# Softmax sums and degrees from a feature set to one, rows turned ahead of their products, and the second expert bias moved into the slots

## The chip, the cores and the metric

The kernel runs on one core of one Trainium2 chip. The metric is the device time of one execution in microseconds (us), the median of several runs. The engines of a core work side by side, each through its own list of instructions: TensorE (PE in the profile, its weight loads PEld), VectorE (DVE), ScalarE (ACT), GpSimd (POOL) and the DMA queues, which are fed from SyncE (SP), ACT and POOL. SBUF is the memory on the core, PSUM the banks into which TensorE writes, DRAM the memory outside.

## What is computed

Four layers with residual sums on 3125 nodes of 256 features and 100,000 edges that are sorted by target node, in float32. The rows are padded to 25 blocks of 128 (3200).

```python
x = x + gnn0(layernorm(x))     # two graph attention layers, 4 heads and 1 head
x = x + ffn0(layernorm(x))     # mixture of 8 experts, 2 chosen for all rows
x = x + gnn1(layernorm(x))     # linear, then two graph convolutions
x = x + ffn1(layernorm(x))     # mixture of 8 experts, 2 chosen for each row

# first attention layer, per head k
h  = x @ W1                                     # 256 -> 4 * 256
e  = leaky_relu((h . a_src)[src] + (h . a_dst)[dst])
w  = exp(e - max of e over the edges into dst)  # a self loop for each node too
out[dst] = sum(w * h[src]) / sum(w)

# graph convolution
deg[dst] = number of edges into dst, plus 1
x  = relu(sum(x[src] @ W / sqrt(deg[src] * deg[dst])) + b)

# last layer, for row n and its two experts e with shares s
y[n] = sum over e of s[n, e] * (gelu(ln_e(x[n]) @ W1[e] + b1[e]) @ W2[e] + b2[e])
```

## The kernel before, in words

`FirstLayer` computes the first attention layer on raw normalised features: the weighted sums of x are made first, and multiplied by W1 afterwards. Its `run` (L2093) begins with a head: it loads all rows, normalises them in groups of five blocks (`norm_rows`, L1541), writes them to a DRAM `table`, multiplies W1 with the attention vectors (`attention_vectors`, L1561), turns every block with PE (L2140), and multiplies each turned block by those vectors (L2148). The scores go to DRAM (`table`, `terms`, `loops`).

Then one loop (L2185) drives three jobs side by side, so many steps of each per turn of the loop. PE, DVE and ACT keep the written order (`in_order`); SP and POOL are ordered by the compiler's scheduler from the dependences.

- Counting (`count_step`): for each of 391 chunks of 256 edges, one-hot tiles are made (L1669 to L1678), multiplied on PE (L1686), and added to a piece of the matrix of edge counts (L1703, L1708). The piece changes nine times (L1659).
- Edges (`edge_step`): for the 283 chunks whose targets lie above node 256. POOL gathers the source rows (L1797, twelve chunks ahead); four chunks are a batch. Per batch, DVE makes the one-hot of target places (`edge_hot`, L1820), the weights `edge_p` (L1840 to L1844), and their product `edge_moves` (L1849), which holds for each row 4 heads x w places, w being 14 or 20. Per chunk, PE multiplies the gathered rows by `edge_moves` for two halves of the features (L1863), and then multiplies `edge_p`, with a fifth column of ones, by `edge_hot` (L1869): that gives the four softmax sums and the degree in five rows. DVE adds the ninefold result to `agg` (L1880): 8 sets of feature sums, and a ninth that is used in its first five rows.
- Dense heads (`dense_step`): targets below 256 are done from the counts, 25 steps a head; `rows` has a 257th column of ones, which gives the sum (L2045).

`agg` covers 384 target nodes at a time, in eight pieces. Work on a finished piece is put in a queue of tasks, and each turn of the loop does one. `new_sums` (L1905) clears a piece and sets the self loops (L1933, and a transpose L1938 and copy L1939 for the ninth set). `through_w1` (L1956) takes the reciprocal of the four sums on four partitions (L1967, L1968), sends it through DRAM so that every partition has it (`by_node`, L1970 and L1975), scales the eight sets (L1982), and multiplies by W1 (L1989). After the last chunk, the last piece's steps up to scaling are put in front of the queue (L2198).

The last layer (`Router`) sends rows to slots. `tasks` (L2311) chooses the experts of each block during the second convolution; its `begin` (L2415) multiplies a block's shares by the experts' second bias (transpose L2419, copy L2421, product L2423, DVE add L2424) and writes the block to the output. The slots (`load`, `front`, `slot`, L2556 to L2638) then each load the weights of one expert, do 256 rows, multiply by the share (L2630), and add the rows to the output by an indirect DMA (L2631). Weights are loaded two slots ahead. Five of the 25 `begin`s run within the first slots.

Of the kernel before, what the change touches and what calls it, by code (L numbers as in the profile page):

```python
# [36 lines left out]
CH = [(c, min(c + 512, NP)) for c in range(0, NP, 512)]  # L37
GB = 5
# [50 lines left out]
class Kernel:  # L89
    def __init__(self, ctx, tc):  # L90
# [10 lines left out]
        self.rows = const.tile([P, NB, D + 1], F32, name="x_rows")  # L101
        self.x = self.rows[:, :, :D]
# [1291 lines left out]
class FirstLayer:  # L1394
# [10 lines left out]
    def __init__(self, k, I):  # L1405
# [8 lines left out]
        self.inverse = k.dram.tile([AS, 4, GA], F32, name="inverse")  # L1414
# [126 lines left out]
    def norm_rows(self, x, to, pool):  # L1541
# [3 lines left out]
        for b in range(GB):  # L1545
            st = pool.tile([P, 6], F32, name="ln0_st", bufs=3)
            nc.vector.bn_stats(st, x[:, b, :])
            nc.vector.bn_aggr(mv[:, b, :], st)
        yield
# [5 lines left out]
        for b in range(GB):  # L1555
            nc.scalar.activation(x[:, b, :], x[:, b, :], AF.Identity, bias=rstd[:, 1, b:b + 1],
                                 scale=rstd[:, 0, b:b + 1])
# [19 lines left out]
    def first_terms(self, sd, pool):  # L1577
# [32 lines left out]
        self.own = pool.tile([P, NB - DB, n + 1], F32, name="own_w")  # L1610
        own = self.own[:, :, :n]
# [4 lines left out]
        nc.vector.memset(self.own[:, :, n:], 1.0)  # L1616
# [136 lines left out]
    def open_sums(self, ctx, w1, stats):  # L1753
# [3 lines left out]
        self.ps_out = ctx.enter_context(tc.tile_pool(name="ps_po1", bufs=DB, space=PSUM, reuse_waits="tile"))  # L1757
# [8 lines left out]
        self.probs = [work.tile([P, BT, 5], F32, name=f"edge_p{i}") for i in range(2)]  # L1766
        for p in self.probs:
            nc.vector.memset(p[:, :, 4:], 1.0)
        self.spread = [work.tile([P, BT * 4 * CW + EW], F32, name=f"edge_moves{i}")
                       for i in range(2)]  # L1770
# [18 lines left out]
        self.hot_e, self.agg = {}, {}  # L1789
        self.ready, self.later = 0, []  # L1790
# [21 lines left out]
    def place_edges(self, m):  # L1812

        nc, work = self.nc, self.work
        n, w = self.size[m], width(C0 + m * BC)
        h = self.hot_e[m] = work.tile([P, BT * CW], F32, name="edge_hot", bufs=3)[
            :, :n * CT * w].rearrange("p (t w) -> p t w", w=w)
# [5 lines left out]
        nc.vector.tensor_scalar(t[:k, :], t[:k, :], self.part[:k, :], None, op0=ALU.is_equal)  # L1823

# [10 lines left out]
    def weigh_edges(self, m):  # L1835
        nc, n = self.nc, self.size[m] * CT
        p = self.probs[m % 2][:, :n, :4]
# [8 lines left out]
    def spread_edges(self, m):  # L1846
        n, w = self.size[m] * CT, width(C0 + m * BC)
        shape = [P, n, 4, w]
        self.nc.vector.tensor_tensor(  # L1849
            self.spread[m % 2][:, :n * 4 * w].rearrange("p (t k w) -> p t k w", k=4, w=w), self.hot_e[m][:, :, None, :].to_broadcast(shape),  # L1850
            self.probs[m % 2][:, :n, :4, None].to_broadcast(shape), ALU.mult)

    def multiply_edges(self, c):
# [6 lines left out]
        for f in range(2):  # L1860
            for u in range(CT):
# [3 lines left out]
                                 rhs=self.spread[m % 2][:, e * 4 * w:e * 4 * w + EW],  # L1865
                                 start=(u == 0), stop=(u == CT - 1))
        for u in range(CT):
            e = q * CT + u
            nc.tensor.matmul(ps[:5, 8 * w:9 * w], lhsT=self.probs[m % 2][:, e, :],  # L1869
                             rhs=self.hot_e[m][:, e, :], start=(u == 0), stop=(u == CT - 1))  # L1870
# [34 lines left out]
    def new_sums(self, q):  # L1905
# [4 lines left out]
        def clear():  # L1910
            a = self.agg[q] = self.work.tile([P, 9, GA + EXT], F32, name="agg1", bufs=2)
            self.nc.vector.memset(a[:, :, n:], 0.0)
            self.nc.vector.memset(a[:, 8, :n], 0.0)
            load(0)
# [12 lines left out]
        def loops(i):  # L1927
            nc, a, k = self.nc, self.agg[q], self.k
# [8 lines left out]
            pt = self.aux.tile([P, 512], F32, name="aux")  # L1937
            nc.tensor.transpose(pt[:5, :P], self.own[:, blocks[i] - DB, :], k.ident)  # L1938
            nc.scalar.copy(a[:5, 8, ts(i, P)], pt[:5, :P])  # L1939
# [16 lines left out]
    def through_w1(self, q):  # L1956
# [5 lines left out]
        inv = []  # L1962

        def invert():
            nc.sync.dma_start(self.deg_row.rearrange("b p -> (b p)")[None, n0:n0 + n],
                              a[4:5, 8, :n])
            nc.vector.tensor_scalar(a[:4, 8, :n], a[:4, 8, :n], 1e-30, None, op0=ALU.max)  # L1967
            nc.vector.reciprocal(a[:4, 8, :n], a[:4, 8, :n])  # L1968

            nc.sync.dma_start(self.inverse[q, :, :n], a[:4, 8, :n])  # L1970

        def load():
            for i in range(0, n, P):
                w = self.work.tile([P, 4 * P], F32, name="by_node", bufs=3)
                nc.sync.dma_start(w.rearrange("p (k n) -> p k n", k=4),  # L1975
                                  self.inverse[q, :, i:i + P][None].to_broadcast([P, 4, P]))
                inv.append(w)

        def scale(i):
            v = a[:, :8, ts(i, P)].rearrange("p (c k) n -> p c k n", c=2)  # L1980
            w = inv[i].rearrange("p (k n) -> p k n", k=4)
            nc.vector.tensor_tensor(v, v, w[:, None].to_broadcast([P, 2, 4, P]), ALU.mult)  # L1982

# [9 lines left out]
        return ([invert, load, lambda: None] + [lambda i=i: scale(i) for i in range(n // P)]  # L1993
# [13 lines left out]
    def open_dense(self):  # L2007
        self.steps = [(h, j) for h in range(4) for j in range(NB)]
        self.cnts, self.t_rows, self.zs, self.ws, self.pos = {}, {}, {}, {}, {}
# [29 lines left out]
    def multiply_dense(self, s):  # L2039
        h, j = self.steps[s]  # L2040
        w = self.ws.pop(s)
        for i in range(DB):
            if j == 0:
                self.pos[i] = self.ps_out.tile([P, 512], F32, name="po")
            self.nc.tensor.matmul(self.pos[i][:, :D + 1], lhsT=w[:, ts(i, P)],  # L2045
                                  rhs=self.k.rows[:, j, :], start=(j == 0), stop=(j == NB - 1))
        if j == NB - 1:
            turned = self.work.tile([P, 2, DN], F32, name="turned")
            for i in range(DB):
                self.dense_end(i, self.pos[i], turned)  # L2050
# [3 lines left out]
    def dense_end(self, i, po, turned):  # L2054
        nc = self.nc
        inv = self.work.tile([P, 1], F32, name="inv", bufs=4)
        nc.vector.tensor_scalar(inv, po[:, D:D + 1], 1e-30, None, op0=ALU.max)
# [692 lines left out]
```

## Time and profile before

| what | us |
|---|---|
| median of 3 runs | 2605.72 |
| lowest and highest run | 2597.94, 2615.81 |
| the profiled execution | 2613.59 |
| its span in the trace | 2611.8 |
| busy in the span: PE, PEld | 2244.2, 1809.0 |
| busy in the span: DVE, ACT, POOL | 1375.9, 1150.3, 821.3 |

The span runs from the first to the last instruction of the trace; the profiled execution's own time is 1.8 us longer. Busy times are averages over stages that differ; the stages are read from stretches of the trace. The head lies from 0 to about 105 us, the loop of the first layer to 1078, its last products to 1112, the second attention layer to about 1500, the chosen experts of the first mixture to about 1720, the convolutions to about 2180, and the slots to the end. The mean granted TensorE clock is 0.904 of full speed. A row such as `L1869 ... x4` stands for merged records; one float32 product has two records, and the bracket at the end of a row gives the idle time before it and what ended it.

### The profile page before, as it was taken

How to read it: one execution, taken by the hardware profiler on the slowest of the kernel's cores; microseconds unless marked ns; L12 is line 12 of the kernel's file. 1: busy time of each engine (PE TensorE's matmuls, PEld its weight loads, DVE VectorE, ACT ScalarE, POOL GpSimd, SP SyncE). 2: the span in 40 equal slices, each digit the busy share in tenths (PEclk: the TensorE clock that was granted, in tenths of full speed). 3: DMA queues.
4: the chain of work that ended last, by engine and by line, in shares of the span. 5: the costliest groups of instructions: out<-in, count | busy, mean ns of one | idle time of the engine just before them, and what ended most of it. 6: DMA issues, size and time to landing. Idle time of an engine off the chain costs nothing. (4 is left out here: it accounts for less than half of the span.)

```text
span 2611.8 us, 38442 instructions
## 1 busy us (share of the span) xinstructions
PE 2244.2 (86%) x11731; PEld 1809.0 (69%) x11731; DVE 1375.9 (53%) x4343; ACT 1150.3 (44%) x2553; POOL 821.3 (31%) x800
## 2 busy tenths in 40 slices
PE   4377878788878888678999979988999998999996
PEld 4255666666656665467888858876877676788886
DVE  7666556466667676613888844342334666111110
ACT  3267555545555555351444424444433444222221
POOL 1555566566566677020000030000000213222221
PEclk8577889888889889889999979999999889799998
DMA  7633445464556556399422110004324435466663
GB/s 231 116 88 84 126 122 169 109 178 114 164 144 181 158 164 177 125 351 304 145 71 76 51 49 1 1 1 139 113 79 155 131 106 195 134 195 196 200 204 77
DMA packets 240363, 354.30 MB, mean 136 GB/s; under 512 B 44640, under 2 KB 181571, under 8 KB 236434
## 3 DMA queue, kind: packets, MB, share of 16 engines
q1 hardware_dynamic: 197122, 252.44, 30.6%
q0 software_dynamic: 39456, 94.80, 14.2%
q10 hardware_dynamic: 3568, 4.47, 0.7%
q8 instruction: 98, 1.61, 0.2%
q14 instruction: 119, 0.97, 0.1%
HBM read 265.94 MB, written 86.20 MB: 135 GB/s over the span
## 5 line engine op out<-in xcount | busy, mean ns | idle before, releaser
L1797 POOL DMA_INDIRECT edge_rows<-table,pick x566 | 604.6, 1068 | 352.2 <-PE edge_sums L1863 139.5
L1863 PE MATMUL edge_sums<-edge_moves,edge_rows 128*128 128x120 f32 x2264 | 357.7, 309 | 36.2 <-DVE agg L1880 23.5
L1863 PEld LDWEIGHTS edge_sums<-edge_moves,edge_rows 128*128 128x128 f32 x2264 | 334.6, 221 | 73.4 <-DVE agg L1880 34.0
L1092 PE MATMUL po<-parts,cnt_r 128*128 128x512 f32 x1250 | 327.7, 416 | 9.5 <-ACT cnt_r L1086 9.5
L1703 ACT CAST acc<-ps 128x325 f32 (+2 forms) x391 | 178.4, 456 | 269.1 <-DVE acc L1708 89.2
L1092 PEld LDWEIGHTS po<-parts,cnt_r 128*128 128x128 f32 x1250 | 240.2, 197 | 69.0 <-ACT cnt_r L1086 10.3
L1686 PE MATMUL ps<-hot_key,hot_lo 128*128 128x350 f16 (+2 forms) x782 | 209.2, 361 | 87.9 <-ACT hot_lo L1678 35.8
L854 PE MATMUL po<-h,w 128*128 128x257 f32 x1250 | 277.6, 382 | 6.7 <-DVE w L845 4.4
L854 PEld LDWEIGHTS po<-h,w 128*128 128x128 f32 x1250 | 236.6, 191 | 43.1 <-DVE w L845 6.4
L1669 DVE TENSOR_SCALAR hot_key<-iota_key,key 128x350 f16<-128x350 f16 (+2 forms) x782 | 231.6, 323 | 24.1 <-PE edge_sums L1863 8.4
L2619 ACT ACTIVATE hid<-ph,ffn_b 128x256 f32<-128x256 f32 (+1 forms) x232 | 105.8, 456 | 278.9 <-PE ph L2617 275.2
L2617 PE MATMUL ph<-xe,ffn_w 128*128 128x256 f32 (+1 forms) x928 | 199.3, 371 | 2.8 <-DMA ffn_w<-in_L_ffn_W 2.8
L2627 PE MATMUL py<-ffn_w,hid 128*128 128x256 f32 x848 | 189.1, 380 | 0.0
L2631 POOL DMA_INDIRECT out<-y,to x53 | 82.6, 1559 | 326.1 <-DVE y L2630 218.0
L2617 PEld LDWEIGHTS ph<-xe,ffn_w 128*128 128x128 f32 x928 | 165.7, 195 | 27.8 <-DVE free L2601 2.9
L2627 PEld LDWEIGHTS py<-ffn_w,hid 128*128 128x128 f32 x848 | 159.2, 191 | 20.4
L839 ACT ACTIVATE z<-z,att_cols 128x640 f32<-128x640 f32 x125 | 103.1, 828 | 152.9 <-DVE z L837 130.1
L1675 ACT ACTIVATE hot_lo<-iota_key,lo 128x128 f16<-128x128 f16 x494 | 169.0, 391 | 0.0
L1880 DVE TENSOR_TENSOR agg<-agg,edge_sums 128x126 f32 (+1 forms) x283 | 87.2, 308 | 148.5 <-remote 41.0
L1686 PEld LDWEIGHTS <-hot_lo 128*128 128x128 f16 x782 | 62.8, 105 | 142.1 <-ACT hot_lo L1678 48.0
L1086 ACT CAST cnt_r<-cnt_h 128x1920 fp32r<-128x1920 f16 x50 | 89.9, 1799 | 136.2 <-PE po L1092 130.8
L2045 PE MATMUL po<-x_rows,w 128*128 128x257 f32 x400 | 128.6, 449 | 2.0 <-issue 2.0
(420 smaller groups left out, 3365.0 us busy)
## 6 DMA issues: line engine op xcount, KB each, us to landing
ffn_w<-in_L_ffn_W SPq DMA_DIRECT2D x58, 1024.0 KB
cnt_h<-cnt SPq DMA_DIRECT2D x50, 800.0 KB
rows<-blank SPq DMA_DIRECT2D x109, 258.0 KB
cnt<-acc SPq DMA_DIRECT2D x50, 400.0 KB
cnt<-cnt SPq DMA_DIRECT2D x25, 800.0 KB
normed<-first_out SPq DMA_DIRECT2D x20, 640.0 KB
first_out<-first SPq DMA_DIRECT2D x56, 192.0 KB
edge_turn<-places SPq DMA_DIRECT2D x283, 32.0 KB
```

The costliest lines, as they stand in the source:

```text
L854: nc.tensor.matmul(pos[i][:, :D + 1], lhsT=w[:, ts(i, P)], rhs=moving[:, j, :D + 1], start=(j == 0), stop=(j == NB - 1))
L1092: nc.tensor.matmul(pos[b], lhsT=c[:, j - j0, ts(b, P)], rhs=parts[i][:, j].rearrange("p a m -> p (a m)"), start=(j == 0), stop=(j == NB - 1))
L1669: nc.vector.tensor_scalar(h[:, u, :NB * w], self.wide[:, :NB * w], self.key[:, t:t + 1], None, op0=ALU.is_equal)
L1675: nc.scalar.activation(l[:, u, :], self.wide[:, :P], AF.Abs, bias=self.lo[:, t:t + 1], scale=-1.0)
L1686: self.nc.tensor.matmul(ps[:, :n], lhsT=l[:, u, :], rhs=h[:, u, :n], start=(u == 0), stop=(u == CT - 1))
L1703: self.nc.scalar.copy(self.acc[g][:, :, ds(o + 1, width(c) - 1)], self.parts[c][:, :, 1:])
L1797: self.nc.gpsimd.indirect_dma_start(out=self.ring[:, e % (RB * BT), :], out_offset=None, in_=self.table, in_offset=bass.IndirectOffsetOnAx ...
L1863: nc.tensor.matmul(ps[:, f * 4 * w:f * 4 * w + EW], lhsT=self.rows_of(m)[:, e, ts(f, P)], rhs=self.spread[m % 2][:, e * 4 * w:e * 4 * w + EW],
L2045: self.nc.tensor.matmul(self.pos[i][:, :D + 1], lhsT=w[:, ts(i, P)], rhs=self.k.rows[:, j, :], start=(j == 0), stop=(j == NB - 1))
L2617: nc.tensor.matmul(ph, lhsT=w1[:, c, ts(f, P)], rhs=xe[:, c, :], start=(c == 0), stop=(c == 1))
L2619: nc.scalar.activation(hid[:, f, :], ph, AF.Gelu, bias=b1[:, f:f + 1])
L2627: nc.tensor.matmul(py, lhsT=hid[:, f, ts(i, P)], rhs=w2[:, f, :], start=(f == 0), stop=(f == NF - 1))
```

## The change

A row that is normalised sums to zero over its 256 features, so the last feature is minus the sum of the others. The change uses that. W1 has its last row subtracted from every row (a 512 KB load of that row to all partitions and a subtraction on POOL), after which the last feature has no weight; that feature is then set to one in the normalised rows. The last partition of each set of feature sums therefore holds the softmax sum of its head, and a fifth set, multiplied by the one-hot alone, holds the degree.

- `edge_moves` gets five sets per row, four weighted and the plain one-hot, in three buffers instead of two; `edge_hot`, the fifth column of `edge_p` and the products at L1869 are gone. The feature products keep 120 columns.
- `new_sums` sets the ninth set to one (self loops) without transposes and copies.
- `through_w1` first sends the four rows of sums from the last partition to a tile of 128 partitions x 12 by four DMAs (`spread`), waits one task, and takes the reciprocal there. There are two tasks more for each piece. After the last chunk, tasks are done until the seventh piece is scaled, and only then the last piece's steps are put in front.
- The dense heads lose the 257th column, and the two blocks of a head share a PSUM bank, so that heads alternate between two banks.
- In the head, all transposes stand ahead of the products with the attention vectors.
- `begin` only writes the block out. Each slot loads its expert's second bias to all partitions (128 KB), and adds it before the share is multiplied.

```diff
+ONE = D - 1
@@ norm_rows
+        nc.vector.memset(x[:, :, ONE:], 1.0)
...
+            nc.scalar.activation(x[:, b, :ONE], x[:, b, :ONE], AF.Identity,
@@ place_edges, spread_edges
-        h = self.hot_e[m] = work.tile([P, BT * CW], F32, name="edge_hot", bufs=3)[
+        h = self.moves(m)[:, :, 4, :]
...
+            t[:, :, :4, :], t[:, :, 4:, :].to_broadcast(shape),
+            self.probs[m % 2][:, :n, :, None].to_broadcast(shape), ALU.mult)
@@ multiply_edges
-                                 rhs=self.spread[m % 2][:, e * 4 * w:e * 4 * w + EW],
+                                 rhs=self.spread[m % 3][:, e * 5 * w:e * 5 * w + EW],
-        for u in range(CT):
-            e = q * CT + u
-            nc.tensor.matmul(ps[:5, 8 * w:9 * w], lhsT=self.probs[m % 2][:, e, :],
-                             rhs=self.hot_e[m][:, e, :], start=(u == 0), stop=(u == CT - 1))
@@ new_sums
-            pt = self.aux.tile([P, 512], F32, name="aux")
-            nc.tensor.transpose(pt[:5, :P], self.own[:, blocks[i] - DB, :], k.ident)
-            nc.scalar.copy(a[:5, 8, ts(i, P)], pt[:5, :P])
@@ through_w1
+        def spread():
+            last = P - 1
+            for h in range(4):
+                nc.sync.dma_start(sums[h * s:(h + 1) * s, :], a[last:, 4 + h, :n])
+            nc.sync.dma_start(self.deg_row.rearrange("b p -> (b p)")[None, n0:n0 + n],
+                              a[last:, 8, :n])
         def invert():
-            nc.vector.tensor_scalar(a[:4, 8, :n], a[:4, 8, :n], 1e-30, None, op0=ALU.max)
-            nc.vector.reciprocal(a[:4, 8, :n], a[:4, 8, :n])
+            nc.vector.tensor_scalar(sums, sums, 1e-30, None, op0=ALU.max)
+            nc.vector.reciprocal(sums, sums)
...
-        return ([invert, load, lambda: None] + [lambda i=i: scale(i) for i in range(n // P)]
+        return ([spread, wait, invert, load, wait] + [lambda i=i: scale(i) for i in range(n // P)]
@@ run
+                nc.gpsimd.dma_start(last_row, bcast(I["L0_gnn_W1"][ONE], 4 * D))
+                nc.gpsimd.tensor_tensor(w1, w1, last_row[:, None, :].to_broadcast([P, 2, 4 * D]),
+                                        ALU.subtract)
...
+                        while self.scaled < AS - 1:
+                            self.tasks.popleft()()
                         last_piece = self.through_w1(AS - 1)
@@ Router.begin
-            nc.tensor.transpose(pt[:8, :P], self.share[:, b, :], k.ident)
-            nc.scalar.copy(sh_t, pt[:8, :P])
-            nc.tensor.matmul(pb, lhsT=sh_t, rhs=self.b2, start=True, stop=True)
-            nc.vector.tensor_add(k.x[:, b, :], k.x[:, b, :], pb)
@@ Router.load, Router.slot
+        nc.sync.dma_start(b2, I["L1_ffn_b2"][ds(e, 1), :].to_broadcast([P, D]))
...
-            nc.vector.tensor_scalar(y, py, xr[:, i, D:D + 1], None, op0=ALU.mult)
+            nc.vector.tensor_add(y, py, b2)
+            nc.vector.tensor_scalar(y, y, xr[:, i, D:D + 1], None, op0=ALU.mult)
```

## The prediction, made before the changed kernel was run

> **What bounds the kernel now.** I read the page's slices first, then the table of busy time by stretch, then the timeline of each engine where the edits lie, and last the lists of waits. The kernel is a chain of stages, and TensorE is the fullest engine in nearly all of them. The loop over counts, edges and dense heads (L2185) runs from about 105 to 1078 us. In the table (PE, PEld, DVE, ACT, POOL busy, then granted clock, DMA share, GB/s) two stretches of it and the second convolution read:
>
> ```profile
> 400.00:500.00 100.00, 82.99 (x535) 63.97 (x534) 60.34 (x223) 53.54 (x145) 63.11 (x61) 0.88 0.51 143
> 900.00:1000.00 100.00, 90.48 (x575) 66.38 (x571) 77.44 (x243) 59.16 (x149) 77.25 (x74) 0.93 0.68 195
> ...
> 2000.00:2100.00 100.00, 93.78 (x413) 69.91 (x413) 63.56 (x238) 43.77 (x74) 19.62 (x20) 0.91 0.43 139
> ```
>
> PE is busy 795 of the loop's 973 us (0.82), DVE 641, ACT 544, POOL 600. PE, DVE and ACT run in program order, so the loop alternates between stretches in which PE never rests and gaps that end when DVE delivers. Both show here:
>
> ```profile
> 880.03 0.26 PE L1869 MATMUL edge_sums<-edge_hot,edge_p 128*5 128x20 f32 x4
> 880.22 1.13 PE L2045 MATMUL po<-x_rows,w 128*128 128x257 f32 x4
> 881.19 0.59 PE L1686 MATMUL ps<-hot_key,hot_lo 128*128 128x500 f16 x2
> 881.62 1.04 PE L1863 MATMUL edge_sums<-edge_moves,edge_rows 128*128 128x120 f32 x8
> 882.60 0.26 PE L1869 MATMUL edge_sums<-edge_hot,edge_p 128*5 128x20 f32 x4
> 882.98 0.58 PE L1686 MATMUL ps<-hot_key,hot_lo 128*128 128x500 f16 x2
> 886.18 0.62 PE L1831 MATMUL aux<-window,edge_turn 128*128 128x16 f32 x4 [2.62 <-DVE edge_turn L1823]
> ```
>
> The reader is to see that L1869 holds PE for 0.19 us a chunk (880.03 to 880.22; the 0.26 overlaps its neighbours), and that the 2.62 us gap is DVE's reciprocal:
>
> ```profile
> 883.15 2.54 DVE L1968 RECIPROCAL agg<-agg 4x384 f32<-4x384 f32 x1
> 885.62 0.25 DVE L1820 TENSOR_TENSOR edge_hot<-place,rel 128x160 f32<-128x160 f32 x1
> 885.80 0.33 DVE L1823 TENSOR_SCALAR edge_turn<-edge_turn,part_place 128x256 f32<-128x256 f32 x1
> ```
>
> The loop ends on a gap too. The seventh piece's products wait behind the last piece's chain through DRAM:
>
> ```profile
> 1077.37 0.58 PE L1686 MATMUL ps<-hot_key,hot_lo 128*128 128x500 f16 x2 [1.62 <-DVE acc L1708]
> 1092.69 19.22 PE L1989 MATMUL ps<-agg,w_all 128*128 128x384 f32 x64 [14.74 <-DVE agg L1982]
> ```
>
> In the second convolution, each block's `begin` cuts into PE's stream, with waits for ACT's copy:
>
> ```profile
> 2161.38 0.95 PE L1092 MATMUL po<-parts,cnt_r 128*128 128x512 f32 x3
> 2163.36 0.69 PE L2423 MATMUL aux<-ffn_b,sh_t 8*128 8x256 f32 x2 [1.02 <-ACT sh_t L2421]
> 2163.98 0.73 PE L1092 MATMUL po<-parts,cnt_r 128*128 128x512 f32 x2
> ```
>
> **The change part by part.** The sum is made against the profiled execution, 2613.6 us (span 2611.8), which is 7.9 us above the median of the three runs.
>
> *A. The sums' products go.* 283 chunks lose L1869; the feature products keep their 120 columns. 283 x 0.19 = 54 us of PE time. Not all counts: in a gap set by DVE, PE only waits longer. The waits show some 90 such gaps (a register load every 8 chunks, "remote" before L1880; 9 turns of the counting piece; 23 L1933; 23 L1982), and each swallows about one chunk's 0.19, 17 us together. I take 0.7 of 54: 38 us. Ends: 16 (0.3 of it) and 54. DVE's copies and products move into one tile of five sets, with the same element counts (L1820 0.31, L1849 0.81 and 0.62 us), and I give the strided rows no cost. Gathers could cap the gain: POOL's own waits for PE (L1863 139.5, L1869 36.5, ps 25.0 us) leave 201 us in all, but only 9 us in 900 to 1000, where A needs some 6.
>
> *B. Reciprocals on 128 rows.* Seven pieces in the loop lose 0.35 + 2.54 us on DVE, and gain about 0.17 + 0.16 (the row of L1552, 128x5): 2.56 x 7 = 18 us. The gaps like that at 886 show that PE feels it. Each piece gains four small DMAs (spread) and two more task turns, and DVE now waits for their landing two turns later, about 5.5 us at 2.75 us a turn. The nearest row is L1982's wait for the write and read of the inverse: 12.8 us in 6 waits, 7.2 of them at the tail, so 5.6 in the loop for two hops. SP issues five DMAs instead of one, 0.24 to 0.3 us each, among windows that are loaded two batches ahead. I take 13. Ends: -5 (each spread as late as those waits) and 18.
>
> *C. Self-loop weights.* 23 transposes L1938 (0.27 us) and copies L1939 (0.25) go, and the one `aux` bank is free for L1831. PE waited for L1939 2.5 us before L1938 and 6.1 before L1831 in the loop. 23 x 0.1 to 0.27 plus 8.6, part of it under L1933 anyway: 8. Ends 2 and 15.
>
> *D. The tail.* All of piece seven's scaling now stands ahead of the last piece's chain, so its eight products (1.29 us each) can start near 1080, not 1092.7. The last chain gains one hop (about 2.1 us, as from the inverse's write at 1080.76 to its read at 1082.90) and loses 1.7 us of reciprocal. Three `ps` and three `first` buffers let six products through before DVE, waiting for the last scale near 1090.5, does their statistics; then 2 x 1.29 + 8 x 0.86 = 9.5 us remain, an end at 1100 where it was 1111.9. I take 12; ends 3 and 16.
>
> *E. `begin` without bias.* 25 transposes, ACT copies (0.25), products and DVE adds (0.42) go. 20 lie in the second convolution: 0.62 + 0.03 us of PE each, 13 us, and 12.0 us of PE idle before L2423. Five lie in the first slots at half clock: 2228.13 to 2243.49 is 15.4 us, of which L2617 fills about 8.9: 6.5. I keep 7 of the 12 idle, as some of it would pass to L1086: 26. Ends 15 and 33.
>
> *F. Bias in the slots.* 29 sure slots get a 128 KB load behind 2 MB of weights, and 53 blocks a second DVE operation. DVE is 17% busy there and PE 100% (2300 to 2500), weights come two slots ahead, and only the last block's extra 0.4 us is on the end. Ends 0 and 14 (3.8 MB at the 200 GB/s seen, 19 us, if three quarters were waited for). I take -0.4, as DMA is 0.69 busy.
>
> *G. The head.* POOL's subtraction of 2048 elements should take 2 x 1.89 (L1434, 1024 elements) = 3.8 us, after 0.5 MB more through DMA that is 0.98 busy (1.7 us at 299 GB/s). W1 is first needed by DVE at 37.87. Behind it on POOL the W2 load (26.47) is needed at 59.2, and the reduction at 66.2. The five small memsets cost 0.3. I take -1; ends 0 and -5.5.
>
> *H, I.* Dense heads alternate banks: L2045 waited 2.0 us in all; I take 1, ends 0 and 5. Turning all rows first: the instruction order was nearly that already (47 transposes before the first product), and DVE works to 64.70 while PE is done at 63.8: 0, ends -1 and 1.
>
> Sum: 38 + 13 + 8 + 12 + 26 - 0.4 - 1 + 1 = 96.6. 2613.6 - 97 = 2517 for an execution like the profiled one; less 7.9, **2510 us**. From the ends, 16 - 5 + 2 + 3 + 15 - 14 - 5.5 + 0 - 1 = 10 to 54 + 18 + 15 + 16 + 33 + 5 + 1 = 142; all ends at once are unlikely.
>
> A rule that speaks against: the loop's granted clock is 0.86, and after an idle of 3.38 us (859.4 to 862.83) the eight records of L1863 took 1.90 us in place of 1.05. The Trainium skill (TensorE: Matmul & The Clock Gate, "HAM oscillation — how this bites in real kernels") says that PE gaps longer than about 3.4 us bring half rate. By that rule, which that row agrees with, A pushes gaps just under the limit over it; as an estimate from the page, five more gaps at about 1.7 us each would make the sum 88 in place of 97.
>
> **The rivals.** *R1: the loop is paced by DVE and ACT, and A vanishes into gaps.* For: 178 us of the loop have no PE work, and 41.0 us of "remote" before L1880 stay. Against: PE runs unbroken for 9 to 10 us at a time between gaps, and DVE waits for it (L1869 38.2, ps 36.1, L1863 14.2 us before L1880). Time: 97 - 38 = 59, so 2547.
>
> *R2, slower: the clock.* Less PE work in the same gaps leaves the loop at a lower granted clock. From 300 to 1050 PE is busy 627 us at 0.89; about 570 would remain. The gain is gone at 570 x (0.89/c - 1) = 97, c = 0.76. At 0.67, midway between 0.74 (150 to 250) and 0.60 (100 to 150), it costs 190: 2700. Against: those low clocks belong to stretches with longer waits, and B to E remove waits.
>
> *R3: no change.* R1 holds, and in the second convolution the converters L1086 and L1087 pace instead (L1086 ended 19.9 us of PE's waits over both layers); only B and D remain, 25: 2581. Against: PE 0.94 busy there.
>
> *R4: more.* The upper ends, with gaps that close and a clock that rises: 142, 2464.
>
> **How the numbers follow.** The forecast holds 0.66, with its own range 2480 to 2535; R1 0.15, R2 0.07, R3 0.05, R4 0.07. The range 2463 to 2562 takes in R1 and leaves out R2, R3 and part of R4, under 0.2. A measurement of this kernel can tell about 1% from no change; the forecast, R1 and R4 are faster by more (0.88), R3 lies within it (0.05), R2 is slower (0.07).
>
> **What would show it.** A: no L1869 rows, L1863 still near 1.05 us for eight, PE busy in the loop about 60 us less and the loop some 60 shorter (R1: some 20 shorter, PE idle up; R2: L1863 at 1.9 and a clock below 0.76). B: the row 128x12 near 0.16 us, and little DVE waiting for the spread DMAs; much waiting would be B's lower end. D: L1989's last block starting soon after the last chunk, its gap well under 14.74. E: the second convolution some 20 us shorter, PE above 0.95. F: L2617 still at 7.1 us for 32 records with no new wait for weights. G: the first count step (51 us) and first gather (77.80) where they were. A gather wait before L1840 well over today's 13.6 us, or new DVE waits on DMA, would make the prediction wrong.

## The result, and the profile after

| | before | changed |
|---|---|---|
| median, us | 2607.34 (4 runs) | 2538.86 (4 runs) |
| lowest and highest, us | 2597.94, 2615.81 | 2525.34, 2545.83 |
| profiled execution, its span, us | 2613.59, 2611.8 | 2545.83, 2544.0 |

The changed kernel takes 0.9732 of the time before (95% interval 0.9674 to 0.979), some 70 us less. The time lies in the range of the prediction (2463 to 2562), 29 us above its 2510. It is 4 us outside the 2480 to 2535 that the forecast itself was given, and 8 below the 2547 of R1.

The two profiled executions are 67.8 us apart. I cut both at the same events, read from the first and last rows of a line on PE (lines of the changed kernel; L1685 is L1686 before, L2623 is L2617, L2633 is L2627), and set the terms of the prediction beside them:

| stretch, from one start of a row to the next | before, us | after, us | gained | forecast |
|---|---|---|---|---|
| head, to the first count step (L1685) | 63.6 | 61.4 | 2.2 | G -1 |
| loop, to the last count step | 1014.0 | 980.4 | 33.6 | A 38, B 13, C 8, H 1: 60 |
| tail, to the second attention layer (L939) | 47.4 | 39.6 | 7.8 | D 12 |
| to the convolutions (first L1092) | 658.4 | 658.2 | 0.2 | 0 |
| convolutions, to the last L1092 | 393.9 | 369.3 | 24.6 | E and F together: 25.6 |
| to the first product of a slot (L2623) | 4.6 | 13.4 | -8.8 | |
| slots, to the last L2633 | 409.2 | 400.8 | 8.4 | |

Nearly all that is missing is missing in the loop (26 us) and in the tail (4). The loop of the kernel before, in the table of busy time by stretch (stretch, its length, then PE, PEld, DVE, ACT, POOL, granted clock, DMA share, GB/s):

```profile
63.60:1077.60 1014.00, 805.03 (x5159) 606.32 (x5159) 668.04 (x2418) 550.60 (x1503) 621.77 (x596) 0.85 0.51 139
```

Of the changed kernel, its whole loop first:

```profile
61.40:1041.80 980.40, 720.79 (x4003) 558.23 (x4004) 648.73 (x2422) 546.54 (x1480) 612.01 (x597) 0.85 0.53 143
400.00:500.00 100.00, 76.78 (x458) 63.43 (x457) 61.71 (x238) 55.50 (x149) 66.02 (x63) 0.90 0.51 142
900.00:1000.00 100.00, 83.14 (x440) 63.32 (x439) 70.93 (x225) 57.20 (x143) 70.44 (x73) 0.88 0.61 174
2000.00:2100.00 100.00, 91.03 (x416) 72.34 (x416) 65.47 (x274) 42.39 (x64) 19.96 (x20) 0.91 0.36 120
```

PE's work in the loop fell by 84 us, but the loop by 34: PE's idle time rose from 209 to 260. PE is now at 0.83 in 900 to 1000, where it was at 0.90. The reciprocal did become short, as B said; this is the timeline of DVE:

```profile
368.03 0.15 DVE L1967 TENSOR_SCALAR edge_p_sums<-edge_p_sums 128x12 f32<-128x12 f32 x1
368.22 0.23 DVE L1968 RECIPROCAL edge_p_sums<-edge_p_sums 128x12 f32<-128x12 f32 x1
```

The tail in the timeline of PE:

```profile
1041.63 0.58 PE L1685 MATMUL ps<-hot_key,hot_lo 128*128 128x500 f16 x2 [0.31 <-DVE acc L1707]
1047.74 10.27 PE L1990 MATMUL ps<-agg,w_all 128*128 128x384 f32 x24 [5.52 <-DVE acc L1707]
1060.97 9.75 PE L1990 MATMUL ps<-agg,w_all 128*128 128x384 f32 x40 [2.96 <-ACT first L2001]
```

And in that of DVE:

```profile
1044.02 3.50 DVE L1982 TENSOR_TENSOR agg<-agg,by_node 128x1024 f32<-128x1024 f32 x3 [2.25 <-DMA by_node<-inverse]
1047.43 0.26 DVE L1707 TENSOR_TENSOR acc<-acc,ps 128x25 f32 x1
1048.40 0.26 DVE L1707 TENSOR_TENSOR acc<-acc,ps 128x25 f32 x1 [0.72 <-ACT acc L1702]
1049.39 0.26 DVE L1707 TENSOR_TENSOR acc<-acc,ps 128x25 f32 x1 [0.72 <-ACT acc L1702]
...
1049.77 0.20 DVE L1968 RECIPROCAL edge_p_sums<-edge_p_sums 128x8 f32<-128x8 f32 x1
1057.53 2.36 DVE L1982 TENSOR_TENSOR agg<-agg,by_node 128x1024 f32<-128x1024 f32 x2 [7.55 <-DMA by_node<-inverse]
```

Six products of the seventh piece now run early, as forecast. But the last piece's reciprocal stands behind the seventh piece's scaling and three adds of the counting, 8.1 us after the last count step (1041.63). Before, it stood 1.6 us after it (1077.37):

```profile
1078.99 1.74 DVE L1968 RECIPROCAL agg<-agg 4x256 f32<-4x256 f32 x1
```

The start of the slots, on PE:

```profile
2099.76 9.49 PE L1092 MATMUL po<-parts,cnt_r 128*128 128x512 f32 x40
2117.60 1.10 PE L2598 MATMUL tr<-ident,xr 128*128 128x128 f32 x4 [8.35 <-DMA xr<-rows]
2122.32 3.75 PE L2623 MATMUL ph<-xe,ffn_w 128*128 128x256 f32 x8 [3.62 <-DMA ffn_w<-in_L_ffn_W]
...
2171.20 9.11 PE L2623 MATMUL ph<-xe,ffn_w 128*128 128x256 f32 x32
```

`begin` is gone from the convolution, and from the first slots. The row at 2171.20 stands where five `begin`s had cut the same 32 records into pieces; before, they took from 2228.30 to 2248.27, 20 us and not 9:

```profile
2228.30 1.06 PE L2617 MATMUL ph<-xe,ffn_w 128*128 128x256 f32 x2
2229.28 1.22 PE L2423 MATMUL aux<-ffn_b,sh_t 8*128 8x256 f32 x2
...
2243.49 4.78 PE L2617 MATMUL ph<-xe,ffn_w 128*128 128x256 f32 x14
```

In exchange there is a wait that no term of mine had. The first slot gathers rows that POOL scatters, and POOL's last scatter starts after the convolution's last product; before, it started at 2170.18, 7 us ahead of the last product's start at 2177.3:

```profile
2111.82 0.96 POOL L2419 DMA_INDIRECT rows<-rt_row,rt_index  x1 [0.30 <-issue]
```

### The profile page after: what moved, and what is told of

Its sections match the earlier page's. It is cut to its first block, busy times and chain, and to the rows that moved or that the text cites. A ratio compares the mean times of both kernels' runs of the same rounds, so it can differ in the third digit from the quotient of the medians.

```text
span 2544.0 us, 36033 instructions
## 1 busy us (share of the span) xinstructions
PE 2125.6 (84%) x10501; PEld 1746.2 (69%) x10501; DVE 1361.0 (53%) x4372; ACT 1138.6 (45%) x2504; POOL 819.5 (32%) x803
## 5 line engine op out<-in xcount | busy, mean ns | idle before, releaser
L1794 POOL DMA_INDIRECT edge_rows<-table,pick x566 | 594.1, 1050 | 329.2 <-issue 116.4
L1864 PE MATMUL edge_sums<-edge_moves,edge_rows 128*128 128x120 f32 x2264 | 362.3, 311 | 66.4 <-issue 33.8
L1864 PEld LDWEIGHTS edge_sums<-edge_moves,edge_rows 128*128 128x128 f32 x2264 | 335.8, 222 | 113.3 <-issue 50.3
L1092 PE MATMUL po<-parts,cnt_r 128*128 128x512 f32 x1250 | 318.3, 410 | 16.7 <-ACT cnt_r L1086 9.5
L1685 PE MATMUL ps<-hot_key,hot_lo 128*128 128x350 f16 (+2 forms) x782 | 210.4, 360 | 125.7 <-ACT hot_lo L1677 51.5
L1092 PEld LDWEIGHTS po<-parts,cnt_r 128*128 128x128 f32 x1250 | 240.1, 195 | 70.4 <-ACT cnt_r L1086 10.3
L1685 PEld LDWEIGHTS <-hot_lo 128*128 128x128 f16 x782 | 76.0, 109 | 183.8 <-ACT hot_lo L1677 68.6
L2623 PE MATMUL ph<-xe,ffn_w 128*128 128x256 f32 (+1 forms) x928 | 194.4, 367 | 3.6 <-DMA ffn_w<-in_L_ffn_W 3.6
L2633 PE MATMUL py<-ffn_w,hid 128*128 128x256 f32 x848 | 189.8, 381 | 1.4 <-ACT hid L2625 1.4
L2623 PEld LDWEIGHTS ph<-xe,ffn_w 128*128 128x128 f32 x928 | 165.1, 194 | 26.9 <-DVE rt_xt L1023 4.0
L2633 PEld LDWEIGHTS py<-ffn_w,hid 128*128 128x128 f32 x848 | 159.3, 191 | 22.2 <-ACT hid L2625 1.8
L1877 DVE TENSOR_TENSOR agg<-agg,edge_sums 128x126 f32 (+1 forms) x283 | 87.2, 308 | 133.0 <-PE ps L1685 35.3
```

Source lines behind the costliest of these rows:

```text
L1092: nc.tensor.matmul(pos[b], lhsT=c[:, j - j0, ts(b, P)], rhs=parts[i][:, j].rearrange("p a m -> p (a m)"), start=(j == 0), stop=(j == NB - 1))
L1685: self.nc.tensor.matmul(ps[:, :n], lhsT=l[:, u, :], rhs=h[:, u, :n], start=(u == 0), stop=(u == CT - 1))
L1794: self.nc.gpsimd.indirect_dma_start(out=self.ring[:, e % (RB * BT), :], out_offset=None, in_=self.table, in_offset=bass.IndirectOffsetOnAx ...
L1864: nc.tensor.matmul(ps[:, f * 4 * w:f * 4 * w + EW], lhsT=self.rows_of(m)[:, e, ts(f, P)], rhs=self.spread[m % 3][:, e * 5 * w:e * 5 * w + EW],
L2623: nc.tensor.matmul(ph, lhsT=w1[:, c, ts(f, P)], rhs=xe[:, c, :], start=(c == 0), stop=(c == 1))
L2633: nc.tensor.matmul(py, lhsT=hid[:, f, ts(i, P)], rhs=w2[:, f, :], start=(f == 0), stop=(f == NF - 1))
```

## The experiments

Each group of four ran on one chip together with the kernel before. The first group is `after_again`, `sums_back`, `sums_twice` and `recip_back`; the second `half_products`, `own_back`, `slot_bias_only` and `flush_only`; the third `before_again`, `sums_double`, `dense_256` and `tail_first`. In the first result and on the chip of the second group the kernel before takes some 2607 us; on the two chips of the first and the third group it takes some 2486. Shares of the kernel before are always taken on the same chip. Within a group two kernels' mean times can also be compared directly, which leaves an uncertainty of 6 to 7 us for six runs each; I give such intervals (95%) and stretches of the profiled executions. A stretch is one execution: the loop of the kernel before took 886.8, 893.3 and 897.0 us in three runs of the third group (unchanged, with narrower dense heads, and with the sums' products doubled).

**The sums' products put back as dead work (A).** Theory P says that the loop is paced by others, theory W that new waits ate the gain. `after_again` is the changed kernel itself, as the base.

> The changed kernel itself once more, as the base of this group. It stood at 0.973 of the kernel before. Two theories of why the loop (first to last step of the count products) got only 34 us shorter though TensorE is busy 83 us less in it. Theory P (pacing): the loop is paced about half by DVE, ACT and the gathers, so any TensorE time taken out comes back as idle time by more than half. Theory W (new waits): TensorE time comes out at about 0.7, as I forecast, and the 20 us that are missing went into new waits, for the spread sums and for the inverse behind them. Both expect 0.968 to 0.978 here, and a loop of 980 us give or take 5.

```diff
@@ multiply_edges, sums_back
+        for u in range(CT):
+            e = q * CT + u
+            nc.tensor.matmul(ps[:4, 400:400 + w], lhsT=self.probs[m % 2][:, e, :],
+                             rhs=self.spread[m % 3][:, (e * 5 + 4) * w:(e * 5 + 5) * w],
+                             start=(u == 0), stop=(u == CT - 1))
@@ sums_twice: the same in a loop of two, into 400 and 440
```

> The changed kernel with the two small products of each chunk put back as dead work (four probabilities against the fifth set, into columns that nobody reads): 54 us of TensorE by the rows of the kernel before. Theory P: 15 to 25 us slower than the changed kernel. Theory W and my forecast: 38 us slower, since the price of the products is what I said and the loss is elsewhere.

> The same with four small dead products a chunk, 108 us of TensorE. Theory P: 35 to 55 us slower than the changed kernel, the second dose dearer than the first as TensorE becomes the bound more often. Theory W: 75 us.

Measured: `after_again` 0.9791 of the kernel before (0.9754 to 0.9827, 2433.80 us), `sums_back` 0.9813 (0.9777 to 0.9848), `sums_twice` 0.9807 (0.9771 to 0.9844). Compared directly, one dose of products costs 7 us (1 to 13) and two doses cost 4 (-4 to 11). The 38 of theory W is excluded, and so are the 15 to 25 and 35 to 55 of theory P. The loop in the table by stretch, for `after_again` (865 us, not the expected 980, as this is another chip):

```profile
61.50:926.50 865.00, 676.58 (x4003) 531.96 (x4004) 644.40 (x2410) 543.73 (x1480) 609.81 (x597) 0.88 0.58 162
```

For `sums_back`:

```profile
61.80:938.30 876.50, 736.89 (x5135) 563.31 (x5136) 647.98 (x2414) 545.04 (x1480) 614.20 (x597) 0.91 0.58 160
```

For `sums_twice`:

```profile
62.00:933.20 871.20, 743.01 (x6268) 575.22 (x6268) 648.77 (x2408) 544.70 (x1480) 611.50 (x597) 0.94 0.58 161
```

Two things hide the work. The first dose makes PE busy for 60 us more, while the loop grows by 11.5 in these executions: 49 us of idle time are filled. The second dose adds 1132 records. It is not worth 54 us of PE: the busy time of the dead products' line goes from 72.7 to 100.9 us, 28 more. And PE as a whole is busy for only 6 us more: the granted clock rises from 0.91 to 0.94 and the two largest lines on PE get faster. The groups of the feature products and count products show both (busy, mean ns of a record, idle time before). In the page of `after_again`:

```profile
L1864 PE MATMUL edge_sums<-edge_moves,edge_rows 128*128 128x120 f32 x2264 | 341.2, 299 | 22.5 <-DVE agg L1877 21.7
...
L1685 PE MATMUL ps<-hot_key,hot_lo 128*128 128x350 f16 (+2 forms) x782 | 202.2, 348 | 119.6 <-ACT hot_lo L1677 61.4
```

Of `sums_back`:

```profile
L1864 PE MATMUL edge_sums<-edge_moves,edge_rows 128*128 128x120 f32 x2264 | 329.7, 292 | 16.3 <-DVE agg L1882 15.6
...
L1685 PE MATMUL ps<-hot_key,hot_lo 128*128 128x350 f16 (+2 forms) x782 | 196.9, 342 | 80.6 <-ACT hot_lo L1677 44.3
```

Of `sums_twice`:

```profile
L1864 PE MATMUL edge_sums<-edge_moves,edge_rows 128*128 128x120 f32 x2264 | 316.9, 285 | 13.6 <-DVE agg L1884 13.0
...
L1685 PE MATMUL ps<-hot_key,hot_lo 128*128 128x350 f16 (+2 forms) x782 | 193.6, 334 | 72.3 <-ACT hot_lo L1677 39.9
```

The reader is to see the idle time ahead of the count products, 119.6, 80.6, 72.3 us, and the mean of a feature product, 299, 292, 285 ns. Against `after_again`, the two lines together are busy for 16.8 us less with the first dose and for 32.9 less with both. Theory W falls with its 38 us. The direction of theory P holds, but its price was too high; that it left out the clock may explain this, and is argued from these rows alone.

**The same from the side of the kernel before.** `before_again` is the kernel before itself, and `sums_double` issues L1869 twice.

> The kernel before once more, for its profile on this chip and for how far two sets of runs of one kernel stand apart: 1.000, with an interval of half a per cent. The group of the dead products ran on a chip on which both kernels were some 5% faster than on the first one, all of it in the loop (865 us where the first chip took 980 for the changed kernel). If the loop of the kernel before takes 1008 to 1018 us here this is a chip like the first; if some 885 to 900, it is one like the second, and the loop gains only 20 to 35 us there by the change.

```diff
@@ multiply_edges, sums_double
+        for u in range(CT):
+            e = q * CT + u
+            nc.tensor.matmul(ps[:5, 400:400 + w], lhsT=self.probs[m % 2][:, e, :],
+                             rhs=self.hot_e[m][:, e, :], start=(u == 0), stop=(u == CT - 1))
```

> The kernel before with the two small products of each chunk issued twice, the second time into columns that nobody reads: 54 us more of TensorE, from the side of the kernel before. By my forecast 38 to 54 us slower than the kernel before. By what the dead products in the changed kernel showed (54 us cost 5, 108 us cost 4, and the mean of an L1864 record fell from 299 to 292 and 285 ns as the granted clock rose): 0 to 10 us slower, the mean of L1863 5 to 10 ns shorter, and the clock in the loop 0.02 to 0.04 higher.

Measured: 1.0003 (0.9983 to 1.0023), and 1.0021 (0.9998 to 1.0043), so 5.2 us with an interval of -0.5 to 10.7: 38 us are excluded from this side too. The loop took 897.0 us, 10 more than in `before_again`, with PE busy for 21 us more. The clock rose less than expected, from 0.90 to 0.91, and the mean of a feature product went from 295 to 292 ns, not 5 to 10 ns down. The loop of `before_again`:

```profile
63.20:950.00 886.80, 747.10 (x5159) 572.17 (x5159) 664.41 (x2418) 546.99 (x1503) 621.64 (x596) 0.90 0.58 159
```

The changed kernel's loop on this chip can be read from `tail_first` below, which alters only the tail: 866.2 us. So the change shortens the loop by 20.6 us here, with PE busy for 68.2 us less (747.10 to 678.94); `after_again`, on a chip of the same speed, has 865.0 and 676.58. Where PE's time went shows in the pages of `before_again` and `tail_first`, in the line of the count products:

```profile
L1686 PE MATMUL ps<-hot_key,hot_lo 128*128 128x350 f16 (+2 forms) x782 | 198.1, 344 | 63.9 <-ACT hot_lo L1678 35.3
...
L1685 PE MATMUL ps<-hot_key,hot_lo 128*128 128x350 f16 (+2 forms) x782 | 203.1, 349 | 116.8 <-ACT hot_lo L1677 67.5
```

The idle time ahead of the count products grew from 63.9 to 116.8 us. These 53 us are close to the 54 at which I had put the sums' products. So PE reaches the next count products sooner and waits there, most of all for ACT's one-hot tile.

**A large dose the other way.**

```diff
@@ multiply_edges, half_products
-        for f in range(2):
+        for f in (1,):
```

> The changed kernel without the products of the features 0 to 127 (the half that holds sums and degrees stays), so these features get their self loops alone: four of the eight records of L1864 a chunk go, some 0.5 us of TensorE each time, 150 us in all; DVE, ACT, the gathers and every DMA stay. A measure of how much the loop follows TensorE. Theory P: 45 to 75 us faster than the changed kernel. Theory W: 100 us or more.

The whole time, 9804 us, says nothing. The slots end near 2504 us, as in the changed kernel, and from 2515 us on the program computes everything once more by its slower general path, which it does when a flag of its own (`doubt`) is set; why the flag was set here was not looked into. The loop does say something: 961.3 us where the changed kernel has 980.4 (and `own_back`, which differs little, 975.7), 14 to 19 us less for about 150 us of PE's work taken out, and less than both theories expected. Its row by stretch:

```profile
61.60:1022.90 961.30, 659.37 (x2871) 451.53 (x2872) 646.19 (x2414) 545.06 (x1480) 607.77 (x597) 0.74 0.54 145
```

The clock fell from 0.85 to 0.74, and the mean record of L1864 took 346 ns, not 311. Only 61 us of busy time went away with half of the feature products. At this rate, 14 to 19 for 150, the sums' 54 us would be worth 5 to 7; this is an estimate, and the only price of PE's work on the slower chip.

**The reciprocal put back (B).**

```diff
@@ through_w1.invert, recip_back
+            nc.vector.tensor_scalar(self.dead[:, :n], self.dead[:, :n], 1e-30, None, op0=ALU.max)
+            nc.vector.reciprocal(self.dead[:, :n], self.dead[:, :n])
```

> The changed kernel with a dead maximum and reciprocal of 4x384 on DVE beside the one of 128x12, right behind it, for every piece: 0.35 + 2.54 us of DVE seven times and 2.0 once at the end. My forecast had 18 us for DVE's part of this, less 5 for new waits. Theory P: 8 to 12 us slower than the changed kernel, as part of it falls where DVE waits anyway. Theory W: 18 to 20 us slower.

Measured: 0.9815 (0.978 to 0.9849), 6 us more than `after_again` (0 to 12). Its loop took 870.9 us, 5.9 more, while DVE was busy for 19.4 us more (663.75 against 644.40). By these two loops about a third of DVE's time came through; W's 18 to 20 did not. The edit also makes a small dead tile, which the lines shown leave out.

**The self-loop transposes put back (C), and the dense heads on 256 columns.** The second is not H itself, which was the alternation of banks; that was not tried alone.

```diff
@@ new_sums.loops, own_back
+            pt = self.aux.tile([P, 512], F32, name="aux")
+            nc.tensor.transpose(pt[:4, :P], self.own[:, blocks[i] - DB, :], k.ident)
+            nc.scalar.copy(self.dead, pt[:4, :P])
...
@@ multiply_dense, dense_256 (on the kernel before)
-            self.nc.tensor.matmul(self.pos[i][:, :D + 1], lhsT=w[:, ts(i, P)],
-                                  rhs=self.k.rows[:, j, :], start=(j == 0), stop=(j == NB - 1))
+            self.nc.tensor.matmul(self.pos[i][:, :D], lhsT=w[:, ts(i, P)],
+                                  rhs=self.k.rows[:, j, :D], start=(j == 0), stop=(j == NB - 1))
...
-        nc.vector.tensor_scalar(inv, po[:, D:D + 1], 1e-30, None, op0=ALU.max)
+        nc.vector.tensor_scalar(inv, po[:, D - 1:D], 1.0, None, op0=ALU.max)
```

> The changed kernel with the 23 transposes of self-loop weights and ACT's copies of them put back as dead work in the one spare bank. My forecast priced these at 8 us (C). Theory W: 8 us slower than the changed kernel. Theory P: 0 to 4.

> The kernel before with its dense heads on 256 columns in place of 257, the banks as they were; the divisor is then the last feature's sum held to at least 1, which is not the softmax sum. The four records of a step took 1.13 us in the kernel before and 1.03 in the changed one, 10 us of TensorE in 100 steps that my forecast did not have (H, 1 us). If TensorE's time counts: 5 to 10 us faster than the kernel before. If the loop gives it back like the sums' products: 0 to 2.

Measured: `own_back` 0.977 (0.9738 to 0.9801); its loop took 975.7 us, not more than the 980.4 of the changed kernel in the first result. Its whole time gives no clear answer: its mean is 9 us above that of the first result (-3 to 21), which may be another chip, and its tail took 43.5 us. So C's 8 us are not seen in the loop, and not excluded in the whole. `dense_256` 1.0004 (0.9985 to 1.0024): the 257th column has no price that shows.

**The slots' bias alone (E and F).** The edit is the last part of the diff, on the kernel before.

> The kernel before with the last part of the change alone: no bias in begin, each slot loads the bias of its expert as 128 rows and adds it on DVE. My forecast had 25.6 us for it (E 26, F -0.4). The profile of the changed kernel shows 24.6 us gained up to the last product of the second convolution, 8.8 lost again before the first slot, 8.4 regained in the first slots. If that loss belongs to this part, 22 to 26 us faster than the kernel before.

Measured: 0.9912 (0.9876 to 0.9947), 23 us. Its stretches: convolutions 365.9 us (28.0 gained), then 13.8 to the first slot (9.2 lost), slots 400.1 (9.1 gained). The late scatter belongs to this part, and so does the gain in the slots.

What became of PE's idle time in the convolutions is seen in the groups of the same stretch, in the first result. Before (1783.4 to 2177.3):

```profile
L1092 PE MATMUL po<-parts,cnt_r 128*128 128x512 f32 x1250 | 327.7, 416 | 9.5 <-ACT cnt_r L1086 9.5
L2423 PE MATMUL aux<-ffn_b,sh_t 8*128 8x256 f32 x40 | 15.6, 474 | 12.0 <-issue 9.0 <-ACT cnt_r L1086 1.4 <-ACT sh_t L2421 1.0
L2419 PE MATMUL aux<-ident,share 128*8 128x128 f32 x20 | 6.2, 308 | 0.0
```

After (1739.6 to 2108.9):

```profile
L1092 PE MATMUL po<-parts,cnt_r 128*128 128x512 f32 x1250 | 318.3, 410 | 16.7 <-ACT cnt_r L1086 9.5 <-DVE o L1107 4.9 <-issue 2.4
```

PE's busy time in the stretch fell by 23.0 us (374.58 to 351.58) and its idle time by 1.6 (19.3 to 17.7). The 12.0 us ahead of L2423 are gone, but 7.2 came back ahead of L1092 and the rest ahead of smaller rows. The granted clock went from 0.94 to 0.96.

**The flush alone (D), and the last reciprocal first.** The first is the kernel before with the two lines of the flush; the second changes the order of the changed kernel:

```diff
@@ run, tail_first
+                        last_piece = self.through_w1(AS - 1)
+                        last_piece.pop(0)()
+                        last_piece.pop(0)
+                        last_piece.pop(0)()
                         while self.scaled < AS - 1:
                             self.tasks.popleft()()
-                        last_piece = self.through_w1(AS - 1)
```

> The kernel before with all scaling of the seventh piece ahead of the last piece's chain, and nothing else of the change. My forecast had 12 us for the tail (D). In the changed kernel the time from the last count step to the first product of the second attention layer fell from 47.4 to 39.6 us, 7.8. If that is the flush alone: 6 to 9 us faster than the kernel before, all of it in this stretch; if the shorter reciprocal did part of it: 4 to 6; by my forecast 12.

> The changed kernel with the last piece's spread and reciprocal issued ahead of the seventh piece's scaling, no longer behind it and behind three count steps: the reciprocal stood at 1049.77 us, 8.1 us after the last count step at 1041.63, where the kernel before had it 1.6 us after. It should start some 5 us sooner, the two scalings of the last piece with it, and the last product end 2 to 4 us sooner; the stretch from the last count step to the second attention layer 36 to 38 us, where it was 39.6. In the whole time 2 to 4 us, too little to tell there. If the last products are held by TensorE alone, nothing.

`flush_only`: 0.9967 (0.9946 to 0.9989), 9 us (3 to 14); the tail took 37.0 us, 10.4 less than before. In the old chain the flush is worth almost what I said, and the changed kernel, at 39.6, seems to lose 2.6 of it. That is little beside the spread: runs that leave the changed tail as it is have 38.2 (`sums_twice`) to 41.7 us (`after_again`). `tail_first`: 0.977 (0.9743 to 0.9797), 2427.62 us, not to be told from `after_again`; its tail took 39.1 us, and not the expected 36 to 38. The reciprocal came 5.4 us after the last count step (at 927.27), not some 3.5; in `after_again` it was 8.5. The timeline of DVE in `tail_first`:

```profile
927.07 0.33 DVE L1877 TENSOR_TENSOR agg<-agg,edge_sums 128x180 f32 x1
932.43 0.17 DVE L1967 TENSOR_SCALAR edge_p_sums<-edge_p_sums 128x8 f32<-128x8 f32 x1 [5.04 <-DMA edge_p_sums<-agg]
932.64 0.20 DVE L1968 RECIPROCAL edge_p_sums<-edge_p_sums 128x8 f32<-128x8 f32 x1
932.76 3.44 DVE L1982 TENSOR_TENSOR agg<-agg,by_node 128x1024 f32<-128x1024 f32 x3
```

The four spread DMAs take 5.0 us from the last add to the landing, not the 2.1 that I had for a hop, and the seventh piece's scaling now waits behind them. A changed kernel without the flush was not tried.

## Why the prediction was right or wrong

*A failed, and it is the step "I take 0.7 of 54: 38 us".* The runs give 5 to 7 us: 5 (-0.5 to 10.7) from the kernel before, 7 (1 to 13) from the changed one. Both were measured on the faster chips; on the slower one there is only the estimate of 5 to 7 from `half_products`. The reading that PE runs unbroken between gaps was right. The conclusion was not: a stretch that ends sooner brings PE sooner to the next gap, and the gap ends when others deliver. The rows name the count products, ahead of which the idle time grew from 63.9 to 116.8 us, most of that in waits for ACT's one-hot tile (35.3 to 67.5). That the gathers hold this chain as well is not shown; DVE's wait for gathered rows ahead of L1840 grew from 13.6 to 19.5 us in the first result, and on the faster chips the kernel before has 35.0 and the changed one 41.6 to 45.7. I had let each gap swallow one chunk's 0.19 us; it can swallow what all chunks since the last gap have saved. So R1, to which I gave 0.15, happened for A, and its time, 2547, is nearer than mine. The profile's own sign of R1, PE idle up, is there with 51 us. That the time came out 8 us below R1 is in part luck: B, C and D came out smaller than R1 counts them, and a part of the loop's gain that no term explains stands in their place (below).

*R2's mechanism took its share.* I asked for a clock of 0.76 before it counts, and the mean of the loop stayed at 0.85. But that mean hides it: the put-back products raise the clock from 0.88 to 0.91 and 0.94, and half of the products fewer lower it to 0.74. The rows show that dead work which fills gaps pays for much of itself in clock. The rule of the Trainium skill (TensorE: Matmul & The Clock Gate, "HAM oscillation — how this bites in real kernels") named the direction, and these rows agree with it. So does the number of PE gaps above 3.4 us, counted from 150 us into the loop: 5 before and 9 after in the first result, 1 in `before_again` and 7 in `after_again`. The 9 us that I had put on it are about right: the lines of the feature and count products became 5.8 us longer from before to after (566.9 to 572.7), and 12.6 from `before_again` to `after_again` (530.8 to 543.4).

The row that I cited for the rule was misread, though. The clock had fallen before the idle of 3.38 us: it is 1.00 from 850.0 to 857.3 us and 0.50 from 857.4 to 867.4, and the idle begins at 859.45.

*B was mis-sized: its 18 us of DVE time measured 6 (0 to 12).* The row is nearly as short as forecast, 0.23 in place of 2.54 us. What failed is that DVE's time counts in full in such a gap; about a third of it did. The 5 us that I took off for new waits depend on the chip: in the loop, the waits for the inverse (L1982) grew from 5.5 to 11.1 us in the first result, but fell from 8.0 to 6.8 from `before_again` to `after_again`. In neither execution of the changed kernel did DVE wait for the spread DMAs in the loop.

*C* (8) shows no price in the loop, and its whole time leaves it open. *H* (1) was not tried alone; the waits of its line on PE are 2.0 us before and 2.1 after. *G and I:* the head was to cost 1 and became 2.2 us shorter, but runs with the old head have 60.3 to 63.6 us, so neither shows.

*What of the loop's gain stays open.* A and B, put back one at a time, make 7 + 6 = 13 us, C and the 257th column nothing that shows in the loop. The loop became some 21 us shorter on the faster chips, 33.6 in the first result. Two executions of one kernel's loop differ by 5 us or more (1008.7 and 1014.0 for the old loop in `slot_bias_only` and before). Parts that are put back singly can each hide in the room that the others left, which would make their sum too small; putting all back together wasn't tried, so this is only argued.

*D was right in size alone (10.4 of 12); in company the tail gave 7.8.* The last piece's scaling, "near 1090.5" and so 13 us after the last count step, came 15.9 us after it in the changed kernel, as the reciprocal stood behind the seventh piece's scaling and three adds. The hop that I had at 2.1 us takes 5.0. That this is what the 2.6 us went to is not shown: with the reciprocal 3 us earlier the tail stayed at 39.1.

*E and F were right as a sum, 24.2 against 25.6, but not as told, so the match is in part luck.* I had 13 us of PE's work and 7 of its idle time for the convolutions. PE's work fell by 23.0 us and its idle time by 1.6: the waits moved to other lines. Another 8.8 us went to a wait for POOL's scatter that I had not named, and the slots gave 8.4 back. Removing work uncovered what it had covered.

## What to carry to other kernels

In a stage where engines wait for each other in turn, a row's duration is not its price: doubling it as dead work costs one run and gives the price of adding it. Here the price of taking it out seemed no higher. Work taken from TensorE in such a stage can come back as idle time and as a lower clock at once, so look for the chain that ends the gaps and shorten that. When an edit removes work ahead of a stage's end, list what that work was covering.

## What the runs showed of the hardware that I had not expected

- The loop of one and the same program took 1014.0 us on one chip and 886.8 on another, while the rest hardly changed (658.4 and 662.1 us from the second attention layer to the convolutions, 409.2 and 411.3 in the slots). On the slower chip, 46.5 us of PE's waits in the loop ended with "issue", that is with nothing that the profile shows, and 0.2 on the other; in the changed kernel 58.8 and 0.6. The cause stays open; it hits this stage alone.
- The granted clock follows gaps that are shorter than I had thought. From 150 us into the loop it fell to half 19 times in `after_again`, and 8 times in `sums_twice`. The Trainium skill (TensorE: Matmul & The Clock Gate, "HAM oscillation — how this bites in real kernels") speaks of gaps of more than about 3.4 us; PE had seven such gaps in `after_again` and one in `sums_twice`, so most of the falls came with shorter ones.
- Four small DMAs from one partition to 128 took 5.0 us from the producer's end to the consumer's start, where the write and the read of the inverse through DRAM took 7.6 together (1049.97 to 1057.53 in the changed kernel).
